# Two interleaved chains of a sequence model: three more handover points, one lead, and issue-order edges for the last causal convolution

## The chip, the core and the metric

The program runs on one core of a Trainium2 chip. The metric is device time in microseconds (us) from start to end of one execution. All data are 32-bit floats. The engines are named as in the profile: PE is TensorE (matrix products), DVE is VectorE, ACT is ScalarE, POOL is GpSimd, SP is SyncE, which here only issues transfers (DMA).

## The reference

The input x has 4 sequences of 512 steps, each step a vector of D = 128 x 64 = 8192. Two layers follow each other. Cut to what matters, with the layer norm written as `ln` and the learned scales left out:

```python
# layer 0, for each sequence
xn = ln(x);  k, v, r = xn @ Wk, xn @ Wv, sigmoid(xn @ Wr)     # 8192 -> 64
s[t] = decay * s[t-1] + k[t] * v[t]                           # scan over time
x = x + (r * s) @ Wo                                          # 64 -> 8192
x = x + gelu(conv3_over_128(ln(x)) + freq_b)                  # 'SAME'
x = x + ln(causal_depthwise_conv3_over_time(ln(x)) + time_b)  # three taps
x = x + gelu(x @ W1 + b1) @ W2 + b2                           # 64 -> 256 -> 64
# layer 1
trend = moving_average(x, 25);  X = rfft(x - trend)[:128]     # over time
y = trend + irfft(einsum(X, complex W per channel))
```

Every `ln` is over all 8192 values of a time step, so its mean and variance are known only when the last channel has been seen.

## The kernel before, in words

Layer 0 holds channels on partitions and the 512 steps in the free dimension. The 8192 channels make 64 tiles of 128, handled in 32 *pairs* (`NPR = 32`), so a tile named `x1`, `z`, `kd` and so on is 128 x 2 x 512. Per sequence `b` there are these stages, each a Python generator that emits instructions and yields a weight:

- **J** `project` (L325): k, v, r and the first statistics, two yields a pair. For b > 1 the weights of two pairs come in one transfer (L351) into a buffer `wx`, of which there are two. `scale_weights` (L355) multiplies them by the norm's scale on DVE (L358). For pair 0 this is free for the planner to place; for later pairs it is tied by `keep_in_program_order`.
- **Z** `scan` (L420): first the statistics of the step (L428 to L433, the last of them on POOL, L234), then `rows` (L281), which spreads a column of 512 values over all partitions by four matmuls (L242) and copies it out on ACT (L286), once for `rs` and once for the mean. Then two products `pk` (L470), one product `pr` (L478), the sigmoid (ACT, L485), the scan (DVE, L489), `rst` (DVE, L491), the product `pq` with `rst` (L496), and a last group `pe` (L504, L505) with the statistics after it. A `yield CHAIN` stands between these groups.
- **A** `attend_and_convolve` (L515): for each pair `attend` (L529 to L535), `convolve` (L550 to L570) and two pairs later `add_up` (L252), the sums for the next statistics. At the end `finish` (L257: the sums copied to s_sb on ACT, `yield CHAIN`, eight small matmuls L264) and `moments` (L272, with POOL's L233 and L234).
- **C** `convolve_time` (L646): `rows`, then for each pair `normed` (two DVE operations, L613 and L616), `tapped` (two ACT L621, four DVE L625, one POOL L631, a store) and its square; PE only has `add_up`, two steps later. Then `finish` and `moments` again. For b = 1 and 2 the first 14 pairs (`AHEAD`) were already made by `convolve_ahead` (L634), inside F of the sequence before.
- **O** `open_feed` (L706): `rows` and the first two residual pairs.
- **F** `feed_forward` (L714): for each pair four quarters `q`, each with one `widen` (L732, gelu on ACT L737) and one `narrow` (L745), then DVE's L758, which empties the two accumulators `p` and `pb` (one bank each, so the next pair's `narrow` waits for it), and a pair or two later `store` (L764, copies L772 and L777). DVE also makes `residual` (L691, L692) and `add_residual` (L703) of the pair two ahead.

**Who sets the order.** PE runs in the order in which the generators emit. `in_turn` (L823) runs two chains, k = 0 and k = 1, side by side through eight pairs of stages (L867 to L874). Each chain has a place `at[k]`: n for the pair of stages, plus a fraction that grows with each yield by weight x share / `whole[stage]`. Chain 1 moves when `at[1] < at[0] + lead`, otherwise chain 0; `lead` runs linearly from `leads[n]` to `leads[n + 1]`. When a stage ends within an entry such as `(C, 0.95), (O, 0.05)`, the generator `run` goes straight on into the next stage; a handover happens only at a yield. `feed_forward` yields after each quarter while the other chain is in a step it called narrow (`CHAIN`), otherwise after each pair.

The queues of DVE, ACT, POOL and SP are ordered by a planner when the program is built: in a simulated run it gives each engine, of what is ready, the instruction that was emitted first. `tc.keep_in_program_order(i)` (in L344, L360, L615, L629, L700) adds one edge: `i` is issued after the instruction emitted just before it on the same engine.[...]

**Layer 1** (L879) starts when layer 0 has ended: transforms, mixing, inverse transforms. The change does not touch it.

Of the kernel before, what the change touches and what calls it, by code (L numbers as in the profile page):

```python
# [24 lines left out]
NPR = NCH // 2  # L25
# [21 lines left out]
def conv_seq_kernel(  # L47
# [26 lines left out]
    x4 = [dram.tile([T, D], F32, tag=f"x4_{b}", name=f"x4_{b}") for b in range(B)]  # L74

    layer0(tc, dram, x, xt, vecs, wkvr, wo, wdec, wconv, fbias, w1, fb1, w2, fb2, x4)
    layer1(tc, x4, wri, dftv, dftd, dfte, idfte, idfto, avg, avgh, out)


@with_exitstack  # L80
def layer0(ctx, tc, dram, x, xt, vecs, wkvr, wo, wdec, wconv, fbias, w1, fb1, w2, fb2, x4):
# [5 lines left out]
    B = x.shape[0]  # L87
# [17 lines left out]
    def two(pool, tag):  # L105
        return pool.tile([P, 2, SL], F32, tag=tag, name=tag)
# [125 lines left out]
    def rsqrt(rs, var):  # L232
        nc.gpsimd.tensor_scalar(rs, var, EPS, None, ALU.add)  # L233
        nc.gpsimd.tensor_tensor(rs, rs, mhalf, ALU.pow)  # L234

    def cols(name):
        return tiny.tile([P, NT], F32, tag=name, name=name)

    def spread(ps, col):

        for t in range(NT):
            nc.tensor.matmul(  # L242
                ps[:, t * P : (t + 1) * P], lhsT=col[:, t : t + 1].to_broadcast([P, P]), rhs=ident,
                start=True, stop=True,
            )

    def add_up(st, i, pair, squares, first, last):

        for j in range(2):
            for k, src in ((0, pair), (1, squares)):  # L250
                q = 2 * j + k
                nc.tensor.matmul(  # L252
                    st[32 * q : 32 * q + 32, :], lhsT=ones, rhs=src[:, j, :],
                    start=first, stop=last,
                )

    def finish(st, bank, tag):  # L257

        s_sb = rowp.tile([P, SL], F32, tag="s", name="s_sb")
        nc.scalar.copy(s_sb, st)  # L260
        yield CHAIN
        pm = bank()
        for t in range(NT):
            nc.tensor.matmul(  # L264
                pm[:, 2 * t : 2 * t + 2], lhsT=s_sb[:, t * P : (t + 1) * P], rhs=pick,
                start=True, stop=True,
            )
        me = tiny.tile([P, NT, 2], F32, tag=f"me{tag}", name="me")
        nc.vector.tensor_copy(me.rearrange("p t k -> p (t k)"), pm[:, 0 : 2 * NT])
        return me[:, :, 0], me[:, :, 1]  # L270

    def moments(mean, square, tag):  # L272

        var, rs, mrs = cols(f"var{tag}"), cols(f"rs{tag}"), cols(f"mrs{tag}")
        nc.vector.tensor_tensor(var, mean, mean, ALU.mult)
        nc.vector.tensor_tensor(var, square, var, ALU.subtract)
        rsqrt(rs, var)
        nc.vector.tensor_tensor(mrs, mean, rs, ALU.mult)
        return rs, mrs

    def rows(bank, a, b, names):  # L281
        both = rowp.tile([P, 2, SL], F32, tag=names, name=names)
        for k, col in enumerate((a, b)):
            pb = bank()
            spread(pb, col)
            nc.scalar.copy(both[:, k, :], pb)  # L286
            yield CHAIN
        return both[:, 0, :], both[:, 1, :]

    def pair_of(row):  # L290
        return row.unsqueeze(1).to_broadcast([P, 2, SL])
# [6 lines left out]
    def spare(tag, n):  # L298
        return fr.tile([P, 2, n], F32, tag=tag, name=tag, bufs={"z": 4, "wx": 2}.get(tag, 3))
# [120 lines left out]
    def scan(b):  # L420
# [13 lines left out]
        if b == 0:  # L434
# [25 lines left out]
            nc.vector.tensor_copy(qo[S:P, 0:S], pq[S:P, 0:S])  # L460
            nc.vector.tensor_scalar_mul(qo[S:P, S:], pq[S:P, S + 2 :], 1.0 / D)
        gw, bw, qo = sums["gw"], sums["bw"], sums["qo"]
        rb, mb = yield from rows(bank, rs, mean, "rm" if b > 1 else "rm3")
        if b == 0:
            kv = two(fr, "x1")
# [138 lines left out]
    def fetch(tag, src, b, i):  # L604
        t = bk.tile([P, 2, SL], F32, tag=tag, name=tag, bufs=3 if tag == "kx" else 2)
        nc.sync.dma_start(t, src[b][2 * i : 2 * i + 2].rearrange("c p t -> p c t"))
        return t


    def normed(b, i, x2, xr, rb, mb, pinned=False):  # L610

        nc.sync.dma_start(x2, x2d[b][2 * i : 2 * i + 2].rearrange("c p t -> p c t"))
        first = nc.vector.tensor_tensor(xr, x2, pair_of(rb), ALU.mult)  # L613
        if pinned:
            tc.keep_in_program_order(first)  # L615
        nc.vector.tensor_tensor(xr, xr, pair_of(mb), ALU.subtract)  # L616

    def tapped(b, i, xr, to, pinned=False):
        for j in range(2):
            c = slice(2 * i + j, 2 * i + j + 1)  # L620
            nc.scalar.activation(  # L621
                to[:, j, :], xr[:, j, :], AF.Identity, bias=tb_all[:, c], scale=vec[:, W2, c]
            )
            for k, w in ((1, W1), (2, W0)):
                tap = nc.vector.scalar_tensor_tensor(  # L625
                    to[:, j, k:], xr[:, j, : SL - k], vec[:, w, c], to[:, j, k:], ALU.mult, ALU.add
                )
                if pinned and j == 0 and k == 1:
                    tc.keep_in_program_order(tap)  # L629
        cc = slice(2 * i, 2 * i + 2)  # L630
        nc.gpsimd.tensor_tensor(to[:, :, 0:2], to[:, :, 0:2], fix[:, cc, :], ALU.add)  # L631
        nc.gpsimd.dma_start(tod[b][cc].rearrange("c p t -> p c t"), to)
# [13 lines left out]
    def convolve_time(b):  # L646
        bank = of_a if b == B - 1 else of_p
        made = AHEAD if b in ahead else 0
        moment = carried.pop(b)
        if made:  # L650
            rb, mb = ahead.pop(b)
        else:
            rb, mb = yield from rows(bank, *moment, "rm" if b == B - 1 else "rm3")
        st = bank()
        waiting, added = [], 0
        n = NPR - made
        for k in range(n + 2):
            while waiting and waiting[0][0] == k - 2:
                add_up(st, 0, *waiting.pop(0)[1:], added == 0, added == NPR - 1)
                added += 1  # L660
            if k < n:
                if b == B - 1:

                    x2, xr, to, sq = spare("xp", SL), spare("x1", SL), spare("z", SL), two(bk, "sq")
                else:
                    x2 = bk.tile([P, 2, SL], F32, tag="kx", name="x2", bufs=3)
                    xr, to = two(bk, "kd"), bk.tile([P, 2, SL], F32, tag="k3", name="to", bufs=3)
                    sq = bk.tile([P, 2, SL], F32, tag="sq4", name="sq4", bufs=2)

                normed(b, made + k, x2, xr, rb, mb, made > 0 and k < 4)  # L670
                tapped(b, made + k, xr, to)
                nc.scalar.activation(sq, to, AF.Square)
                waiting.append((k, to, sq))
                i = k * made // n
                if i != (k + 1) * made // n:

                    to = fetch("kh", tod, b, i)
                    sq = bk.tile([P, 2, SL], F32, tag="mid", name="sq5", bufs=4)
                    nc.scalar.activation(sq, to, AF.Square)
                    waiting.append((k, to, sq))  # L680
            yield 7.0 * (NPR + 2) / (n + 2)
        mean, sq = yield from finish(st, bank, 4)
        causal[b] = moments(mean, sq, 4)


    def residual(b, i):
# [123 lines left out]
    CHAIN = 6.0  # L810
# [40 lines left out]
    def nothing(b):  # L851
        yield 1.0

    J, Z, A, C, O, F = project, scan, attend_and_convolve, convolve_time, open_feed, feed_forward
    begin[A] = 0
    needed = {A: scanned, C: carried, O: causal, F: opened}
    whole = {
        J: 2.0 * NPR, Z: 7 * CHAIN, A: 7.0 * NPR + 3 * CHAIN, C: 7.0 * (NPR + 2) + 3 * CHAIN, O: 4 * CHAIN,
        F: 9.0 * (NPR + 1), nothing: 1.0,
    }  # L860
    with tc.manual_schedule(engines={nc.tensor.engine}):
        for _ in project(0):
            pass
        prepare()
        in_turn(
            (0.12, 0.12, 0.08, 0.1, 0.08, 0.1, -0.05, 0.08, 0.0),
            ((0, (Z, 0.12), (A, 0.88)), (1, (J, 0.88), (Z, 0.12))),  # L867
            ((0, (C, 1.0)), (1, (A, 1.0))),
            ((0, (O, 0.05), (F, 0.95)), (2, (J, 0.88), (Z, 0.12))),
            ((1, (C, 1.0)), (2, (A, 1.0))),  # L870
            ((1, (O, 0.05), (F, 0.95)), (3, (J, 0.88), (Z, 0.12))),
            ((2, (C, 1.0)), (3, (A, 1.0))),
            ((2, (O, 0.05), (F, 0.95)), (3, (C, 0.95), (O, 0.05))),
            ((3, (F, 1.0)), (3, (nothing, 1.0))),  # L874
        )
# [321 lines left out]
```

## Time and profile before

| | |
|---|---|
| three runs | 3748.67, 3748.59, 3736.15 us; median 3748.59 |
| the profiled execution | 3734.79 us, its span from first to last instruction 3733.0 us |
| mean granted PE clock | 0.981 |
| layer 0 ends (last `store`) | about 2752 us |

The stretches of layer 0, from the windows of the profile, with the stages that run side by side (n is the pair of stages):

| n | stretch, us | stages | PE busy, us | DVE busy, us |
|---|---|---|---|---|
| 0 | 210 to 520 | A0 with J1, Z1 | 298.35 | 173.47 |
| 1 | 520 to 795 | C0 with A1 | 251.14 | 262.29 |
| 2 | 795 to 1225 | O0, F0 with J2, Z2 | 404.51 | 293.35 |
| 3 | 1225 to 1450 | C1 with A2 | 215.80 | 200.93 |
| 4 | 1450 to 1890 | O1, F1 with J3, Z3 | 418.24 | 300.22 |
| 5 | 1890 to 2122 | C2 with A3 | 223.87 | 200.43 |
| 6 | 2122 to 2487 | F2 with C3, O3 | 323.70 | 326.00 |
| 7 | 2487 to 2752 | F3 | 262.22 | 150.49 |

A line of the timeline gives the start, the time from start to end, the engine, the line of the kernel, the operation, output<-inputs, their shapes and how many instructions are merged; in brackets stands how long the engine had been idle before it and what ended that. A 32-bit matmul of the program shows as two PE instructions.

### The profile page before, as it was taken

What the parts mean: (1) busy time and instruction counts of PE and PEld (TensorE: products, weight loads), DVE (VectorE), ACT (ScalarE), POOL (GpSimd) and SP (SyncE); (2) the same over time, 40 slices, a digit from 0 to 9 for tenths busy, and PEclk for the clock granted to TensorE, in tenths of its full rate; (3) what the DMA queues carried; (4) which work ended last, traced back from release to release, by engine and by line L of the source; (5) the groups of instructions that cost most, each with busy time, mean ns of one, the idle gap of its engine ahead of it and who ended that gap; (6) DMA issues with size and microseconds to landing.
All of it is one profiled execution on the core that took longest, in us unless ns stands there. A gap on an engine that the chain in (4) does not pass through costs nothing. (4 is left out here: it accounts for less than half of the span.)

```text
span 3733.0 us, 53000 instructions
## 1 busy us (share of the span) xinstructions
PE 3521.2 (94%) x20041; PEld 1360.6 (36%) x20041; DVE 2671.9 (72%) x3498; ACT 1778.0 (48%) x2331; POOL 447.3 (12%) x654
## 2 busy tenths in 40 slices
PE   9999999999998999999989989999989999989998
PEld 4433322234333223433322233333323843328533
DVE  4455569976776896676789699946658277792677
ACT  0012346655656565565656578868854200152100
POOL 0000012210101221001122122100000000001000
PEclk9999999999999999999999999999999999999999
DMA  9867657787874687788578677645569478894687
GB/s 314 279 211 242 227 177 262 260 276 265 290 262 168 235 280 271 266 292 278 182 238 286 213 247 267 234 149 196 198 203 287 150 240 290 290 297 164 213 294 260
DMA packets 427223, 910.29 MB, mean 244 GB/s; under 512 B 32728, under 2 KB 83160, under 8 KB 422872
## 3 DMA queue, kind: packets, MB, share of 16 engines
q1 hardware_dynamic: 353136, 636.92, 52.5%
q0 software_dynamic: 71680, 268.46, 19.7%
q8 instruction: 160, 2.62, 0.3%
q10 hardware_dynamic: 2152, 1.51, 0.1%
q14 instruction: 95, 0.78, 0.1%
HBM read 638.26 MB, written 268.50 MB: 243 GB/s over the span
## 5 line engine op out<-in xcount | busy, mean ns | idle before, releaser
L745 PE MATMUL p<-mid,w_sb 64*64 64x512 f32 x2048 | 554.5, 599 | 20.3 <-DVE wx L758 20.3
L745 PE MATMUL pb<-mid,w_sb 64*64 64x512 f32 x2048 | 536.2, 598 | 0.0
L737 ACT ACTIVATE mid<-c,fb_sb 128x1024 f32<-128x1024 f32 x256 | 284.3, 1111 | 97.2 <-PE c L732 94.8
L737 ACT ACTIVATE mid<-m,fb_sb 128x1024 f32<-128x1024 f32 x256 | 284.6, 1112 | 93.5 <-PE m L732 92.1
L732 PE MATMUL c<-x,w_sb 64*64 64x512 f32 x2016 | 281.2, 611 | 13.2 <-ACT mid L737 6.9
L732 PE MATMUL m<-x,w_sb 64*64 64x512 f32 x2016 | 283.0, 612 | 6.7 <-ACT ob L777 4.9
L745 PEld LDWEIGHTS p<-mid,w_sb 64*64 64x64 f32 x2048 | 155.5, 135 | 294.9 <-issue 262.0
L409 PE MATMUL a<-xp,wx 128*128 128x512 f32 x512 | 242.6, 617 | 9.1 <-DVE wx L358 8.6
L1043 ACT COPY two<-a 128x512 f32<-128x512 f32 x64 | 37.5, 585 | 428.9 <-PE a L1038 428.9
L1066 PE MATMUL b<-xin,avg_sb 128*128 128x512 f32 x512 | 230.8, 593 | 3.3 <-DVE xin L1072 3.3
L1072 DVE TENSOR_TENSOR xin<-b,pm 128x512 f32<-128x512 f32 x256 | 159.1, 683 | 100.2 <-PE b L1069 85.3
L570 ACT ACTIVATE sq<-x 128x1024 f32<-128x1024 f32 x128 | 135.1, 1055 | 181.4 <-DVE x L567 181.3
L625 DVE SCALAR_TENSOR_TENSOR to<-kd,vec,to 128x510 f32<-128x510 f32 (+1 forms) x272 | 197.1, 744 | 9.8 <-ACT to L621 8.7
L700 ACT ACTIVATE kd<-kd,vec 128x512 f32<-128x512 f32 x256 | 192.8, 803 | 3.1 <-DVE kd L692 3.1
L252 PE MATMUL st<-x,ones 128*32 128x512 f32 x512 | 176.8, 603 | 13.1 <-DVE x L567 13.1
L925 DVE COPY xf<-b 128x256 f32<-128x256 f32 x128 | 54.4, 425 | 178.3 <-PE b L1012 169.4
L625 DVE SCALAR_TENSOR_TENSOR z<-x,vec,z 128x511 f32<-128x511 f32 x240 | 175.9, 745 | 5.3 <-ACT z L621 3.0
L531 DVE TENSOR_TENSOR x<-a,xp 128x1024 f32<-128x1024 f32 x128 | 156.1, 1220 | 30.6 <-PE a L529 28.4
L703 DVE TENSOR_TENSOR x<-kd,kx 128x1024 f32<-128x1024 f32 x126 | 154.1, 1223 | 32.8 <-ACT kd L700 32.7
L529 PE MATMUL a<-rst,wo_sb 64*128 64x512 f32 x512 | 147.0, 648 | 27.1 <-DVE x L531 25.1
L758 DVE SCALAR_TENSOR_TENSOR x4t<-p,fb_sb,x 128x512 f32<-128x512 f32 x64 | 47.9, 748 | 172.0 <-PE pb L745 169.6
L692 DVE TENSOR_TENSOR kd<-kd,rm 128x1024 f32<-128x1024 f32 x128 | 155.7, 1220 | 7.8 <-ACT rm L286 6.3
(269 smaller groups left out, 6755.1 us busy)
## 6 DMA issues: line engine op xcount, KB each, us to landing
xp<-in_xt SPq DMA_DIRECT2D x256, 512.0 KB
kh<-to SPq DMA_DIRECT2D x156, 512.0 KB
x<-x POOLq DMA_DIRECT2D x128, 512.0 KB, 4.6
kx<-x SPq DMA_DIRECT2D x128, 512.0 KB
x<-ob POOLq DMA_DIRECT2D x64, 1024.0 KB, 8.0
xin<-x SPq DMA_DIRECT2D x64, 1024.0 KB
out<-xin POOLq DMA_DIRECT2D x64, 1024.0 KB, 6.6
x<-x SPq DMA_DIRECT2D x96, 512.0 KB
```

The lines of the kernel that those rows point to most:

```text
L252: nc.tensor.matmul(st[32 * q : 32 * q + 32, :], lhsT=ones, rhs=src[:, j, :], start=first, stop=last,)
L409: nc.tensor.matmul(pa[:, k, :], lhsT=wq[:, j, k * P : (k + 1) * P], rhs=xp[:, j, :], start=first and j == 0, stop=last and j == 1,)
L531: nc.vector.tensor_tensor(x1, at, xp, ALU.add)
L625: tap = nc.vector.scalar_tensor_tensor(to[:, j, k:], xr[:, j, : SL - k], vec[:, w, c], to[:, j, k:], ALU.mult, ALU.add)
L692: nc.vector.tensor_tensor(d, d, pair_of(mb), ALU.subtract)
L700: tc.keep_in_program_order(nc.scalar.activation(d[:, j, :], d[:, j, :], AF.Identity, bias=vec[:, B4, c], scale=vec[:, G4, c]))
L703: nc.vector.tensor_tensor(x3, d, x2, ALU.add)
L732: nc.tensor.matmul(pm[halves[j], h, :], lhsT=w1_sb[halves[h], q * H : (q + 1) * H], rhs=x3[halves[h], j, :], start=True, stop=True,)
L737: nc.scalar.activation(mid, pm, AF.Gelu_apprx_tanh, bias=fb1_sb[:, q : q + 1])
L745: nc.tensor.matmul(sums2[i][j][halves[h], :], lhsT=w2_sb[halves[j], q, :], rhs=mid[halves[j], h, :], start=q == 0, stop=q == 3,)
L1066: nc.tensor.matmul(po[j], lhsT=avg_sb[:, j, :], rhs=xin[:, j, :], start=True, stop=False)
L1072: nc.vector.tensor_tensor(by_n(xin[:, j, :]), by_n(po[j]), by_c(pm[j % 2][:, j // 2, :]), ALU.add)
```

## The change

Four edits:

1. In `convolve_time`, `normed` and `tapped` of the last sequence (b = 3) get `keep_in_program_order` on their first DVE instruction (the first of the taps in `tapped`); in `normed` the condition `made > 0` stays in front.
2. In `scan`, a `yield CHAIN` between the statistics and `rows`; in `convolve_time`, a `yield CHAIN` after the last `moments`.
3. `whole` counts the new yields: Z has 8 instead of 7, C has 4 instead of 3.
4. The lead at the border from pair 5 to pair 6 goes from -0.05 to -0.1.

```diff
         gw, bw, qo = sums["gw"], sums["bw"], sums["qo"]
+        yield CHAIN
         rb, mb = yield from rows(bank, rs, mean, "rm" if b > 1 else "rm3")
...
-                normed(b, made + k, x2, xr, rb, mb, made > 0 and k < 4)
-                tapped(b, made + k, xr, to)
+                normed(b, made + k, x2, xr, rb, mb, made > 0 and (k < 4 or b == B - 1))
+                tapped(b, made + k, xr, to, b == B - 1)
...
         causal[b] = moments(mean, sq, 4)
+        yield CHAIN
...
-        J: 2.0 * NPR, Z: 7 * CHAIN, A: 7.0 * NPR + 3 * CHAIN, C: 7.0 * (NPR + 2) + 3 * CHAIN, O: 4 * CHAIN,
+        J: 2.0 * NPR, Z: 8 * CHAIN, A: 7.0 * NPR + 3 * CHAIN, C: 7.0 * (NPR + 2) + 4 * CHAIN, O: 4 * CHAIN,
...
-            (0.12, 0.12, 0.08, 0.1, 0.08, 0.1, -0.05, 0.08, 0.0),
+            (0.12, 0.12, 0.08, 0.1, 0.08, 0.1, -0.1, 0.08, 0.0),
```

## The prediction

> **What bounds the kernel now.** I read the page's busy times first, then PE's waits, the windows, and PE's and DVE's timelines where the waits lie.
>
> ```profile
> PE 3521.2 (94%) x20041; PEld 1360.6 (36%) x20041; DVE 2671.9 (72%) x3498; ACT 1778.0 (48%) x2331; POOL 447.3 (12%) x654
> PE p L745 <- DVE wx L758: 20.3, 7, 5.8
> PE a L242 <- POOL rs L234: 12.3, 6, 4.0
> PE p L242 <- POOL rs L234: 4.2, 2, 2.1
> ```
>
> PE is busy 94%: a step that is reordered pays only by idle time of PE. The waits (total, times, longest) say what the handovers can reach: the spreads of `rows` wait for POOL's L234 16.5 us in all, in eight places. Where they are, in PE's timeline:
>
> ```profile
> 810.57 1.85 PE L242 MATMUL p<-ident,rs 128*128 128x128 f32 x8 [2.08 <-POOL rs L234]
> 1141.94 1.16 PE L242 MATMUL a<-ident,rs 128*128 128x128 f32 x8 [1.91 <-POOL rs L234]
> 1807.68 1.16 PE L242 MATMUL a<-ident,rs 128*128 128x128 f32 x8 [1.63 <-POOL rs L234]
> 2127.19 2.07 PE L242 MATMUL a<-ident,rs 128*128 128x128 f32 x8 [3.41 <-POOL rs L234]
> 2460.93 2.08 PE L242 MATMUL a<-ident,rs 128*128 128x128 f32 x8 [4.03 <-POOL rs L234]
> 2462.80 1.92 PE L764 MATMUL m<-ident,wx 128*128 128x128 f32 x8
> ```
>
> These are O0, Z2, Z3, C3 and O3; the other three, at C0, A1 and A0, follow `moments` of A or the end of Z, where nothing is added. After the longest waits PE runs at half speed: the spread takes 2.08 us instead of 1.16, the transposes 1.92 instead of 1.09.
>
> Pair 6 is different, as the windows show (length, then PE, PEld, DVE, ACT, POOL busy, the granted PE clock, the DMA share, GB/s):
>
> ```profile
> 2300.00:2350.00 50.00, 45.17 (x372) 17.25 (x368) 49.69 (x58) 43.23 (x54) 9.68 (x13) 0.97 0.80 257
> 2600.00:2650.00 50.00, 50.00 (x448) 19.51 (x444) 30.51 (x30) 41.20 (x46) 2.27 (x3) 1.00 0.59 198
> ```
>
> While C3 runs beside F2, DVE is full (49.69 of 50) and PE waits for it now and then; when F runs alone PE is full. Removing a wait of PE in the first kind of window gains nothing by itself.
>
> [...] The trace agrees on the half (above), and shows it after 2.31 us of idleness too (1833.62: the next L732 group takes 1.97 us, not 1.04). [...] at 1174.15 below, ready DVE work stands behind one that waits. [...] the trace has 1.28 before the sigmoid L485.
>
> **The change, part by part.** I worked `in_turn` through with both sets of fractions to see which emission moves.
>
> *The edges: nothing.* `made` is 14 only for b = 1 and 2, so for b = 3 `made > 0` is false and `normed` is not tied. In `tapped` the instruction emitted just before the first tap is L616 of the same pair, whose output the tap reads. The edge is there already. 0 us; no reason for a gain or loss.
>
> *Z0.* One half-step of J1 goes between statistics and spread. The idle time there is 0.73 us (180.88, waiting for DVE L461), but J1 waits 3.65 us for its weights at 192.56, which may eat it: -0.4, from -0.7 to 0.
>
> *Z1.* No idle time at its spread now: no gain. But its later steps move. Z's steps were 0.12/7 = 0.0171, and are 0.015. Chain 1 starts at 0.88, so `pr` is emitted at 0.955 and `pq` at 0.97; with lead 0.12 they need at[0] > 0.835 and > 0.85. A's steps (0.88/242 a unit weight) take at[0] from 0.833 to 0.851 in one `convolve`: both conditions come true at once, and `pr` and `pq` stand next to each other. Before, an `attend` and a `convolve` (some 5 us) lay between, and still:
>
> ```profile
> 467.47 0.74 DVE L483 SCALAR_TENSOR_TENSOR rg<-rm,gw,p 128x512 f32<-128x512 f32 x1
> 470.92 1.22 DVE L489 TENSOR_TENSOR_SCAN state<-decb,wx 128x512 f32<-128x512 f32 x1
> 473.17 0.69 DVE L491 TENSOR_TENSOR rst<-rg,state 128x512 f32<-128x512 f32 x1
> 473.91 1.07 PE L496 MATMUL p<-rst,qo 64*64 64x512 f32 x2 [2.02 <-DVE rst L491]
> ```
>
> `pr` ended at 467.1, `rst` at 473.86: 6.8 us with L531 and L535 between. DVE's own operations are 0.74 + 0.69 + 0.48 + 0.74 + 1.22 + 0.69 = 4.6; with one foreign one (1.1) 5.7 us of idle PE, and some 2.2 us from the half clock (after 4.03 at 2460.93 three groups took 5.9 us instead of 3.3, 2.6 more). 7.9 - 2.0 = +5.9, from 0 to +9. Everything of A0 and A1 is queued behind `pq` on PE.
>
> *C0 to O0.* A half-step of J2 (four products of the program, about 2 us) comes between `moments` and the spread: -2.0 of 2.08, from -2.1 to 0. For C1 to O1 there was no wait. A step of C shrinks from 7/256 to 7/262 of the stage, so C runs slightly further ahead of A in pairs 1, 3, 5; DVE does the same work, 0.
>
> *Z2.* A `store` and a quarter of F0 (over 3 us) cover its spread: -1.9. There is a second effect, in DVE's queue:
>
> ```profile
> 1169.50 1.22 DVE L489 TENSOR_TENSOR_SCAN state<-decb,wx 128x512 f32<-128x512 f32 x1
> 1174.15 0.55 DVE L358 TENSOR_SCALAR wx<-wx,vec 128x192 f32<-128x192 f32 x2 [3.42 <-DMA wx<-in_wkvr]
> 1174.61 0.74 DVE L758 SCALAR_TENSOR_TENSOR x4t<-p,fb_sb,x 128x512 f32<-128x512 f32 x1
> 1175.50 1.09 PE L764 MATMUL c<-ident,x4t 128*128 128x128 f32 x4 [4.71 <-DVE x4t L758]
> ```
>
> L358 here scales the weights of J3's pair 2, nearly 300 us before J3: it is tied to that of pair 1, which is tied to that of pair 0, which is free, so all three float up. It waits for a transfer into the `wx` buffer that the scan held till L489, and PE waits behind L758. With the new fractions the `moments` of C1 (DVE's L278) are emitted just before pair 2's scaling; the tie then holds it to its place. L758 would start near 1170.8 and leave about 0.95 us of PE idleness, as at the later stores (1201.55). Gain 4.71 - 0.95, the second wait of 0.61, and about 1.9 of half clock: -6.3. The transfer itself is still issued and may hold SP's queue. Against it, `pr` to `pq` have only two quarters (4.3 us) between them instead of a `store` and two: `rst` needs 0.7 + 0.7 on DVE, a table load 1.28 and the sigmoid 0.72 on ACT, 0.7 on DVE, waits and one or two foreign operations: 6.5 us, so +2.2. Sum -6.0, from -8.2 to 0.
>
> *Z3.* -1.6 at the spread, and +1.4 at `pq` (2.2 where 0.77 is now): -0.2, from -3 to +4.
>
> *The border and pair 6.* With the lead at -0.1, O2's `rows` and the first pair and a quarter of F2 come before A3's last `moments`. What PE now idles for A3's statistics at 2122.73 (0.71) goes. But `moments` of A3 and the spread of C3 stay adjacent (A ends without a yield), so the 3.41 stays, later: F2 starts at 2122 instead of 2129, C3's DVE work not at 2130.7 but after two `widen`, 1.5 us for the gelu, five quarters of 2.15, L264, the 3.41 and the spread: near 2142.5. From there I count DVE: successive starts in the timeline are 1.13 us for a 1024-wide operation (three L616 from 2137.82 take 3.50 us together) and 0.66 for a tap, so a C3 pair is 2 x 1.13 + 4 x 0.67 = 4.94, a pair of F2 3 x 1.13 + 2 x 0.66 = 4.73. An F2 pair outside the overlap costs PE's 8.93 us (80 instructions a pair at 448 in 50 us). Before: 24 pairs of F2 have their L758 by 2399, so 2130.7 + 32 x 4.94 + 24 x 4.73 + 8 x 8.93 = 2473.7. After: C3's steps run at 1.33 a pair instead of 1.2 and end one pair of F2 earlier, so 21.7 pairs overlap, 1.25 lie ahead: 2142.5 + 158.1 + 102.6 + 80.8 = 2484.0. +10.3. The waits at L745 in this stage (20.3 us) are DVE being full, and I count no gain there. Fewer `add_up` stand in F2's tail (its pairs take 9.5 there, now 8.93): -1.2. And O3: two quarters, a `store` and another quarter cover its statistics: -4.0 and -2.6 of half clock. Sum +2.5, from -8 to +10.
>
> **Sum:** -0.4 + 5.9 - 2.0 - 6.0 - 0.2 + 2.5 = -0.2 us. On the profiled execution, 3734.8 us (span 3733.0 and 1.8 around it), that is 3734.6. The three runs lie at 3748.6 twice and 3736.2; their mean is 3744.5, the median 4 us higher. I predict 3744. The bounds of the terms add to -22 and +23: 3722 to 3767.
>
> **Rivals.** *A, most of the idleness goes.* If the planner reorders DVE in pair 6 so that L758 never waits, all that the handovers and the lead can touch is gone: 2.1 + 1.9 + 1.6 + 0.7 + 3.4 + 4.0, 6.3 at Z2, L745's waits at the border 3.72 + 5.83, and some 8 of half clock: -37.5, and Z1 doesn't grow: 3707. For it: those waits are long. Against: DVE at 49.69 of 50.
> *B, C3 comes late (slower).* DVE is the bound of pair 6, and each F2 pair pushed out of the overlap costs 8.93 - 4.73 = 4.2 us. My +10.3 counts 2.3 such. Five more are +21 and the sum +20.8: 3765. It decides (over 0.5%) from 18.9 / 4.2 = 4.5 pairs beyond mine, that is with C3's first L613 past 2142.5 + 4.5 x 8.93 = 2183; with Z1 at its upper bound from 3.8. For it: the last `moments` of A3 need three small DVE slots among F2's work. Against: they are emitted early and so come first. C3's loads (L612 on SP) also stand behind those of three more F2 residuals (L606), and its stores (L632 on POOL) come later; I count 0 for both, as loads run pairs ahead and the transfer share is 0.80 there; if that cover fails, L613 waits for its load and this rival has its cause.
> *C, all is hidden anyway:* the moved waits reappear at the next wait (J's weights, `p`'s bank), and Z1's five microseconds are taken from A0's own waits: 3745.
>
> Chances: forecast 0.57, A 0.2, B 0.11, C 0.12. Since 0.5% (18.7 us) is about what a measurement of this kernel can tell from no change, forecast and C count as the same: 0.69; faster 0.2, slower 0.11. The range takes the bounds, a little of A: 3720 to 3765.
>
> **What would show it.** `pq` of Z1 with 5 to 6 us of idleness; no L358 waiting near 1174; no wait at the spreads of Z2, Z3, O0, O3; one of about 3.4 us at C3, after a pair of F2; C3's L613 near 2142; DVE's order within a C3 pair unchanged. The prediction is wrong if `pr` and `pq` are apart in PE's order, if L758 in pair 6 stops waiting, or if F2's end moves by more than 10 us.

## The result, and the profile after

The changed kernel takes 3754.9 us (median of 9 runs, 3749.6 to 3758.6), the kernel before 3737.2 beside it (9 runs, 3726.4 to 3748.7). The ratio is 1.0035, with a 95% interval of 1.0022 to 1.0048: 13.1 us slower, 8.2 to 17.9. (The medians alone lie 17.7 us apart; the text uses the ratio on record.) The profiled execution took 3749.6 (span 3747.8), 14.8 more than that of before. The handovers are two new yields, although the title counts three.

The busy times of the page and the waits of PE (total, times, longest) after the change:

```profile
PE 3530.2 (94%) x20041; PEld 1358.5 (36%) x20041; DVE 2670.0 (71%) x3498; ACT 1781.6 (48%) x2331; POOL 447.1 (12%) x654
PE st L252 <- DVE x L568: 19.6, 21, 3.7
PE p L747 <- DVE wx L760: 18.3, 7, 4.3
PE m L734 <- ACT mid L739: 10.8, 8, 6.4
PE p L497 <- DVE rst L492: 6.9, 1, 6.9
PE a L242 <- POOL rs L234: 5.0, 3, 3.8
PE p L242 <- POOL rs L234: 2.4, 2, 2.1
```

The code lines have moved by one from the scan on and by two after the convolution (L745 is L747 now, L758 is L760). The spreads of `rows` wait 7.4 us instead of 16.5: the handovers did what they say. But new rows stand beside them: `pq` of Z1 waits 6.9 us, the column sums `st` of A 6.5 us more than before (13.1), and `widen` waits 10.8 us for ACT at its bank `m`, where it was 1.6, most of it in F2. L747's wait for DVE (L760) has hardly changed. PE's timeline at the places that the prediction showed, in order Z1, Z2, Z3, A3's end, C3's spread, F2:

```profile
478.15 1.96 PE L497 MATMUL p<-rst,qo 64*64 64x512 f32 x2 [6.88 <-DVE rst L492]
1145.25 1.00 PE L766 MATMUL c<-ident,x4t 128*128 128x128 f32 x6 [1.53 <-DVE x4t L760]
1173.57 0.66 PE L766 MATMUL c<-ident,x4t 128*128 128x128 f32 x2 [5.93 <-DVE x4t L760]
1807.06 1.11 PE L766 MATMUL c<-ident,x4t 128*128 128x128 f32 x7 [1.53 <-DVE x4t L760]
1832.73 1.23 PE L766 MATMUL c<-ident,x4t 128*128 128x128 f32 x8 [3.29 <-DVE x4t L760]
2132.05 1.91 PE L252 MATMUL st<-x,ones 128*32 128x512 f32 x2 [3.71 <-DVE x L568]
2152.66 2.07 PE L242 MATMUL a<-ident,rs 128*128 128x128 f32 x8 [3.76 <-POOL rs L234]
2180.69 1.13 PE L734 MATMUL m<-x,w_sb 64*64 64x512 f32 x4 [6.37 <-ACT mid L739]
```

No spread of O0, Z2, Z3 or O3 waits any more; at Z2 and Z3 a wait of 1.53 us at the next `store` stands in its place. C3's spread waits about as long as before (3.76 us for 3.41), 25 us later. In the windows of pair 6 nothing is new, DVE is full while C3 runs (49.69 of 50) and PE when it has ended:

```profile
2300.00:2350.00 50.00, 44.20 (x356) 18.07 (x360) 49.69 (x57) 41.47 (x51) 9.70 (x13) 0.97 0.78 257
2600.00:2650.00 50.00, 49.82 (x444) 19.36 (x440) 31.27 (x32) 40.72 (x47) 2.36 (x4) 1.00 0.56 191
```

To see where the time went I took, in both traces, the time from the start of an instruction of PE to that of a later one (the k-th of its kind), how much of it PE idled, and how much the halved clock took (half of the stretches in it with a granted clock of 0.5). The table gives the differences to the kernel before, and already those of the three single parts from the experiments below: total (idle, clock).

| stretch | after | scan alone | convolution alone | lead alone |
|---|---|---|---|---|
| A0's attend 24 to A1's attend 8 (with Z1) | +10.6 (+4.9, +6.8) | +7.5 (+4.9, +5.1) | +12.8 (0, +15.4) | 0 (0, 0) |
| J2's start to F0's first narrow (O0) | -4.6 (-1.8, -1.7) | -1.7 (0, -1.7) | -4.6 (-1.8, -1.7) | 0 |
| F0's pair 24 to J3's start (Z2, pair 3) | -3.5 (-1.9, -6.8) | -4.3 (-2.7, -5.1) | -3.6 (-2.5, -6.8) | -3.8 (-0.2, -5.1) |
| F1's pair 24 to A3's attend 0 (Z3) | +0.7 (+0.5, 0) | +0.7 (+0.4, 0) | +0.4 (+0.5, 0) | 0 |
| A3's attend 0 to its last convolve (pair 5) | +9.4 (-0.8, +5.1) | +1.5 (-0.9, +5.1) | +7.0 (-1.2, +12.0) | +10.5 (+2.7, +5.1) |
| from there to F2's first narrow | -4.1 (-1.1, 0) | 0 | -0.2 (+0.4, -1.7) | -5.1 (-0.7, -1.7) |
| F2's pairs 0 to 15 | +18.9 (+10.7, +5.1) | +0.1 | +3.3 (+1.9, 0) | +15.9 (+8.1, +6.8) |
| F2's pairs 16 to 31 (with O3) | -6.4 (-4.1, -3.4) | -1.6 (-0.1, -1.7) | -10.8 (-6.7, -3.4) | -3.8 (-3.1, -1.7) |

Rows five and six belong together: after the change, and with the lead alone, O2's rows are emitted ahead of A3's last convolve and so count in row five. The clock column has to be read with care: the convolution alone loses 15.4 us at Z1, where its instructions are those of the kernel before, and the lead alone has -3.8 in row three, where it changes nothing. What that is comes first among the experiments.

### The profile page after: what moved, and what is told of

It is laid out like the page before. It is cut to its first block, busy times and chain, and to the rows that moved or that the text cites. A ratio compares the mean times of both kernels' runs of the same rounds, so it can differ in the third digit from the quotient of the medians.

```text
span 3747.8 us, 52999 instructions
## 1 busy us (share of the span) xinstructions
PE 3530.2 (94%) x20041; PEld 1358.5 (36%) x20041; DVE 2670.0 (71%) x3498; ACT 1781.6 (48%) x2331; POOL 447.1 (12%) x654
## 5 line engine op out<-in xcount | busy, mean ns | idle before, releaser
L747 PE MATMUL p<-mid,w_sb 64*64 64x512 f32 x2048 | 558.7, 600 | 19.1 <-DVE wx L760 18.3
L747 PE MATMUL pb<-mid,w_sb 64*64 64x512 f32 x2048 | 534.6, 599 | 0.0
L734 PE MATMUL m<-x,w_sb 64*64 64x512 f32 x2016 | 280.3, 610 | 15.5 <-ACT mid L739 10.8
L734 PE MATMUL c<-x,w_sb 64*64 64x512 f32 x2016 | 280.9, 611 | 10.8 <-ACT mid L739 7.3
L747 PEld LDWEIGHTS p<-mid,w_sb 64*64 64x64 f32 x2048 | 156.8, 135 | 292.7 <-issue 257.8
L626 DVE SCALAR_TENSOR_TENSOR to<-kd,vec,to 128x511 f32<-128x511 f32 (+1 forms) x272 | 195.9, 749 | 9.4 <-ACT to L622 8.4
L760 DVE SCALAR_TENSOR_TENSOR x4t<-p,fb_sb,x 128x512 f32<-128x512 f32 x64 | 47.9, 748 | 182.7 <-PE pb L747 182.7
L569 POOL DMA_DIRECT2D x<-x x128 | 93.6, 731 | 568.9 <-DVE x L568 558.9
```

The lines of the kernel that those rows point to most:

```text
L626: tap = nc.vector.scalar_tensor_tensor(to[:, j, k:], xr[:, j, : SL - k], vec[:, w, c], to[:, j, k:], ALU.mult, ALU.add)
L734: nc.tensor.matmul(pm[halves[j], h, :], lhsT=w1_sb[halves[h], q * H : (q + 1) * H], rhs=x3[halves[h], j, :], start=True, stop=True,)
L747: nc.tensor.matmul(sums2[i][j][halves[h], :], lhsT=w2_sb[halves[j], q, :], rhs=mid[halves[j], h, :], start=q == 0, stop=q == 3,)
```

## The experiments

Ratios are to the kernel before, run beside each; in us they are multiplied by 3739. My theory before the experiments: the loss sits in two places, at Z1 (the scan's handover) and at the border of pairs 5 and 6 (the lead). The rival: it is all in pair 6, where DVE is full.

**The edges alone.**

```diff
-normed(b, made + k, x2, xr, rb, mb, made > 0 and k < 4)
-tapped(b, made + k, xr, to)
+normed(b, made + k, x2, xr, rb, mb, made > 0 and (k < 4 or b == B - 1))
+tapped(b, made + k, xr, to, b == B - 1)
```

> The two edges alone. Both theories: the instruction order of every engine is that of the kernel before, so the ratio is 1.000; what it differs by, and where the two traces part by chance of the granted clock, is what a difference of a few us means in this study (expected: within 0.1%, 4 us, and single profiles apart by up to 7 us).

Measured 0.9998 (0.9986 to 1.0009). The instructions of all five engines are the same and in the same order, so this is a second profile of the kernel before. Yet in pair 5 it is 3.7 us longer, with 5.1 us more lost to the clock and 0.6 us less idle. That is the size of chance in one profile and one stretch. In pair 5 it is one-sided: the traces of seven kernels in which DVE has the same order there as before (the edges, the scan, its two halves, and below C3's handover, that without C2, and C3's spread covered) are all 1.5 to 4.9 us longer from A3's attend 0 to its last convolve. The profile of the kernel before is a fast one there, and some 3 us of each figure for pair 5 belong to that. Chance can be larger. Windows of the kernel before, and then of the convolution alone, at the end of Z1 (length, PE, PEld, DVE, ACT, POOL, granted clock, DMA share, GB/s):

```profile
474.00:504.00 30.00, 27.55 (x157) 9.78 (x158) 15.24 (x20) 11.20 (x17) 4.34 (x6) 1.00 0.40 134
```

```profile
474.00:504.00 30.00, 28.06 (x100) 9.23 (x101) 10.08 (x17) 6.21 (x9) 2.78 (x4) 0.60 0.28 92
```

The pause before both is the same, 2.02 us at `pq` (473.91 and 474.16), in the same order of work. In one execution the clock stays whole, in the other it is halved for 13.65 us and soon again for 10.24, and the 30 us hold 100 matmuls instead of 157. So single profiles serve here for idle time and its place, and the runs for sums.

**The three parts, each alone.**

```diff
+        yield CHAIN                    # scan, ahead of rows
-Z: 7 * CHAIN
+Z: 8 * CHAIN
```

> The handover in scan alone (Z counted as 8 steps). Theory 1 (the loss sits at Z1 and at the border of pairs 5 and 6): +9.5 us stand by the end of chain Z1, nothing at O0 and O3, the spreads of Z2 and Z3 give back 1 to 2 us each, the long wait at the identity copies of x4t in Z2 for the third weight pair stays; sum +6 to +9, ratio 1.0016 to 1.0024. Theory 2 (the loss is all in pair 6, where DVE is full; what stands at Z1 is eaten later): -2 to +2 us at the end.

```diff
+        yield CHAIN                    # convolve_time, after moments
-C: 7.0 * (NPR + 2) + 3 * CHAIN
+C: 7.0 * (NPR + 2) + 4 * CHAIN
```

> The handover after a convolution's moments alone (C counted with 4 chain steps). Theory 1: -4 us at O0, -5 at Z2 (the third pair's scaling no longer waits on DVE ahead of the store's), -6 to -8 at O3, pair 6 otherwise as before; sum -12 to -18, ratio 0.9952 to 0.9968. Theory 2: C's smaller steps put more of C's DVE work beside F2 late, PE's waits at the narrow products grow by 10 us or more in pair 6; sum 0 to +5.

```diff
-(0.12, 0.12, 0.08, 0.1, 0.08, 0.1, -0.05, 0.08, 0.0)
+(0.12, 0.12, 0.08, 0.1, 0.08, 0.1, -0.1, 0.08, 0.0)
```

> The lead of -0.1 at the border of pairs 5 and 6 alone. Theory 1: A3's end shows an idle PE of 3 to 4 us at the column sums of its last pair (no spread of O2 left to cover it), the 3.4 us wait at C3's spread stays, and F2's tail ends later; +6 to +12 us, ratio 1.0016 to 1.0032, all of it after 2100 us. Theory 2: +12 to +18 us, most of it in waits of PE for ACT or DVE within F2's first five pairs.

| part | ratio (95%) | us | my prediction's terms |
|---|---|---|---|
| scan | 1.0015 (1.0005 to 1.0025) | +5.6 | -0.4 + 5.9 - 1.9 + 2.2 - 0.2 = +5.6 |
| convolution | 0.9977 (0.9966 to 0.9989) | -8.6 | -2.0 - 6.3 - 6.6 = -14.9 |
| lead | 1.0044 (1.0031 to 1.0057) | +16.5 | +10.3 - 1.2 = +9.1 |

Edges and parts together are +12.8, the change +13.1: on the whole they add up. The scan's term held as a sum (that it fits to the tenth is luck, the interval is 1.9 to 9.3, and of its parts Z2 went another way, below), the lead costs nearly twice what I had, and the convolution gives 6 us less. Of the expectations, the scan came just under theory 1's range; the convolution fell between the two, and theory 2's growing waits are not there; the lead's 16.5 lies in theory 2's range, not in mine, although theory 1's idle PE at A3's sums is in its trace (3.71 us).

**Scan's two halves.** The handover for b < 2 only, with eight steps for these two chains, and for b > 1 only, with seven as before:

```diff
+        if b < 2:                      # the other kernel: if b > 1
+            yield CHAIN
-weight * share / whole[stage]
+weight * share / (8 * CHAIN if stage is scan and b < 2 else whole[stage])    # b < 2 only
```

> The handover in scan for b < 2 only, with eight steps for these two chains and seven for Z2 and Z3 as before. Theory 1: Z1's pq shows 6 to 7 us of idle PE and half clock after it; +5 to +9 us, ratio 1.0013 to 1.0024. Theory 2: -1 to +2 us, ratio 0.9997 to 1.0005.

Measured 1.0022 (1.0009 to 1.0036), +8.2 us: theory 1. `pq` of Z1 in its timeline, and then what DVE did in the changed kernel between `pr`'s end (471.25) and `rst`:

```profile
480.97 1.96 PE L498 MATMUL p<-rst,qo 64*64 64x512 f32 x2 [7.17 <-DVE rst L493]
```

```profile
471.25 1.21 DVE L490 TENSOR_TENSOR_SCAN state<-decb,wx 128x512 f32<-128x512 f32 x1
472.39 0.72 DVE L484 SCALAR_TENSOR_TENSOR rg<-rm,gw,p 128x512 f32<-128x512 f32 x1
473.03 1.21 DVE L568 TENSOR_TENSOR x<-m,x 128x1024 f32<-128x1024 f32 x1
474.16 0.68 DVE L485 TENSOR_TENSOR rg<-rg,rm 128x512 f32<-128x512 f32 x1
475.83 0.55 DVE L358 TENSOR_SCALAR wx<-wx,vec 128x192 f32<-128x192 f32 x2 [0.99 <-DMA wx<-in_wkvr]
477.40 0.69 DVE L492 TENSOR_TENSOR rst<-rg,state 128x512 f32<-128x512 f32 x1 [1.02 <-ACT rg L486]
```

One foreign operation (L568), as I had counted, and the sigmoid's way over ACT, which I had not put into Z1's sum: L358 with its 0.99 us of waiting fits into that. PE idles 6.88 us instead of the 5.7 forecast.

> The handover in scan for b > 1 only, Z's steps as before, nothing else. Theory 1 (scan's loss is Z1, where pr and pq become neighbours): -1 to -4 us, ratio 0.9989 to 0.9997. Theory 2 (in Z2 and Z3 the wait at the spread comes back at the identity copies of x4t and at ACT's mid, with more behind it): +3 to +8 us, ratio 1.0008 to 1.0021.

Measured 1.0035 (1.0018 to 1.0052), +13.1 us, above both theories. This kernel is not what the change does to Z2 and Z3: with eight steps of a seventh each the chain ends later, and A's spread comes right behind it. Its timeline at Z3:

```profile
1840.77 1.97 PE L766 MATMUL m<-ident,x4t 128*128 128x128 f32 x8 [4.40 <-ACT mid L739]
1854.27 2.08 PE L242 MATMUL a<-ident,rs 128*128 128x128 f32 x8 [2.09 <-POOL rs L234]
```

The trace has +5.6 us at Z3 (idle +2.8, clock +5.1); its runs have the lowest mean clock of all (0.976, before 0.980). So the share per step matters too, not the handover alone. The same edit on top of the convolution's:

> The handover after a convolution's moments, and that in scan for b > 1 only, with Z's steps as before: Z0 and Z1 are emitted as in the kernel before, the lead is -0.05, no edges. Theory 1: the convolution's -8.6 and 1 to 4 us at Z2 and Z3: -9 to -13 us, ratio 0.9965 to 0.9976. Theory 2 (Z2 and Z3 have nothing to give once the convolution hands over): -8.6 us, ratio 0.9977.

1.0002 (0.9990 to 1.0014): both theories missed, the handover at this share takes back what the convolution's gave.

**The change without the lead.**

```diff
-(0.12, 0.12, 0.08, 0.1, 0.08, 0.1, -0.1, 0.08, 0.0)
+(0.12, 0.12, 0.08, 0.1, 0.08, 0.1, -0.05, 0.08, 0.0)     # rest as changed
```

> The whole change except the lead, which stays at -0.05. Theory 1 (the parts add up; the lead is the loss): +5.6 for scan and -8.6 for the convolution, together -3 us, ratio 0.9987 to 0.9997. Theory 2 (the two handovers give back part of each other's gain in pair 6): +3 to +8 us, ratio 1.0008 to 1.0021.

Measured 1.0010 (0.9995 to 1.0024), +3.7 us: at the low end of theory 2's range; the interval (-1.9 to +9.0) just reaches theory 1's. Theory 2's reason is not in the trace: from A3's last convolve to F3 it has -9.2 us, the whole gain. Against the change's 1.0035 that leaves 9 us, give or take 7, for the lead in the company of the rest.

**The lead's two halves.** `in_turn` interpolates: `lead = leads[n] + (leads[n + 1] - leads[n]) * (at[0] - n)`. The entry for the border is also the end of pair 5's slope, so C2's pairs are emitted up to two of A3's `convolve` earlier. My prediction had looked at the border only.

```diff
+            if n == 5:
+                lead -= 0.05 * (at[0] - 5)       # pair 5 only
```

> The lead is interpolated over pair 5 towards its value at the border, so -0.1 also shifts C2 against A3 all through pair 5. Here only that part: the lead goes to -0.1 over pair 5, and pair 6 has its old leads. Theory 1 (half of the lead's cost lies in pair 5, where DVE's order changes from A3's attend 8 on): +5 to +9 us, ratio 1.0013 to 1.0024. Theory 2 (all of it lies at the border and in pair 6): -1 to +3 us, ratio 0.9997 to 1.0008.

```diff
+            if n == 6:
+                lead -= 0.05 * (7 - at[0])       # pair 6 only
```

> The other part: pair 5 has its old lead up to -0.05, and pair 6 starts at -0.1. Emission at the border and in pair 6 as with the whole lead. Theory 1: +5 to +10 us, ratio 1.0013 to 1.0027 (C3 starts some 16 us late against A3's end, and pair 6 ends 7 to 9 later). Theory 2: +14 to +18 us, ratio 1.0037 to 1.0048.

Pair 5 alone: 1.0019 (1.0010 to 1.0029), +7.1 us, theory 1. Its trace has +8.0 from A3's attend 0 to its last convolve (idle +2.0, clock +3.4), some 3 of it chance as above, and nothing at the border. DVE takes C2's work in another order, and one `attend` of A3 waits longer for L531, 3.14 us instead of 2.09:

```profile
1949.85 1.13 PE L529 MATMUL a<-rst,wo_sb 64*128 64x512 f32 x4 [3.14 <-DVE x L531]
```

That is not the loss, though: all waits of `attend` for L531 in this stretch take 7.2 us here and 7.4 before, and in the changed kernel PE idles 0.8 us less in pair 5 than before. So the 7.1 us are shown by the runs; in which wait they lie is not shown.

Pair 6 alone: 1.0036 (1.0022 to 1.0050), +13.5 us, just under theory 2's range. Its trace has +7.2 from A3's last convolve to F3, and +6.7 before it, where O2's rows now stand right behind C2's `moments`, with a halved clock after the pause (the second spread takes 2.08 us, the first 1.16; some 3 us are the chance in pair 5, and the next stretch, which has lost O2's rows, is 4.9 shorter):

```profile
2111.38 1.16 PE L242 MATMUL p<-ident,rs 128*128 128x128 f32 x8 [2.10 <-POOL rs L234]
2113.21 2.08 PE L242 MATMUL p<-ident,mrs 128*128 128x128 f32 x8 [0.68 <-ACT rm L286]
```

The 2.10 us are this kernel's own: with the whole lead, alone or in the change, C2 ends earlier and O2's first spread doesn't wait (its second waits 0.71 us, as before). The two halves, 7.1 and 13.5, therefore need not add to the lead's 16.5; what is left of it beside pair 5 is 9.4.

**What a late C3 costs.** Three more kernels move the border. In the first, O2's rows wait under the full lead until A3's last convolve is emitted; in the second the lead is 0; in the third (with the convolution's handover for C3 alone, below) C3 yields once before its rows, so that a whole pair of F2 covers its spread.

```diff
+        while b == B - 2 and not summed[0]:      # open_feed; summed is set after A3's last convolve
+            yield BLOCKED
```

> The lead of -0.1 alone, but O2's rows are held back until A3's last convolve is emitted, so that its spreads and residuals cover A3's last column sums again, as before the change. Theory 1 (C3 starts late and its work on DVE ends late, and that is the price): at most the 3.7 us of idle PE and some 2 us of half clock go, +10 to +14 us remain, ratio 1.0027 to 1.0037. Theory 2 (A3's uncovered sums and the clock after them are the price): +2 to +6 us, ratio 1.0005 to 1.0016.

```diff
-(0.12, 0.12, 0.08, 0.1, 0.08, 0.1, -0.05, 0.08, 0.0)
+(0.12, 0.12, 0.08, 0.1, 0.08, 0.1, 0.0, 0.08, 0.0)
```

> The kernel before with a lead of 0 at the border instead of -0.05: A3's end and C3's rows come ahead of O2's residuals and of F2. Theory 1 (every us by which C3 starts later costs about one): C3 starts 5 to 8 us earlier against A3's end, -3 to -7 us, ratio 0.9981 to 0.9992. Theory 2 (the order at the border itself decides, and -0.05 is where O2 covers A3's sums): A3's sums and both spreads stand bare, +3 to +8 us, ratio 1.0008 to 1.0021.

```diff
+            if b == B - 1:                       # convolve_time, ahead of rows
+                yield BLOCKED
```

> The handover for C3 alone, and C3 yields once before its rows, so that a whole pair of F2 stands on PE between A3's last statistics and C3's spread; C3's first pair keeps its place in PE's order, the lead is -0.05. Theory 1 (the bare spread is worth its 3.4 us and some 2 us of half clock, and C3's later first pair costs at most one pair of F2 outside the overlap, 4.2 us): -9 to -13 us against the kernel before, ratio 0.9965 to 0.9976. Theory 2 (every us by which C3 starts later is lost again in pair 6): -3 to -7 us, ratio 0.9981 to 0.9992.

Holding O2 back: 1.0049 (1.0030 to 1.0069), +18.3, theory 1 or worse. A lead of 0: 1.0034 (1.0019 to 1.0049), +12.7, on theory 2's side and above its range. C3's spread covered: 1.0001 (0.9989 to 1.0012), +0.4, worse than both theories and 8 us behind the same kernel without that yield. From the traces, us after the start of the last bias product of A3's last convolve:

| kernel | C3's first `normed` on DVE | F2's first narrow | F3's first narrow |
|---|---|---|---|
| before | 16.8 | 19.4 | 376.8 |
| C3's handover | 16.8 | 19.4 | 367.5 |
| the same, C3's spread covered | 26.9 | 17.3 | 376.8 |
| lead, pair 6 only | 30.7 | 14.5 | 383.9 |
| lead alone | 30.6 | 14.3 | 383.7 |
| lead, O2 held back | 33.4 | 17.2 | 386.5 |
| lead of 0 | 21.0 | 29.1 | 383.5 |
| changed kernel | 31.6 | 15.3 | 385.2 |

Rows two and three differ in C3's rows alone: C3 10.1 us later, the end 9.3 us later, although the spread doesn't wait any more:

```profile
2141.48 1.16 PE L242 MATMUL a<-ident,rs 128*128 128x128 f32 x8
2161.18 1.99 PE L736 MATMUL c<-x,w_sb 64*64 64x512 f32 x8 [6.09 <-ACT mid L741]
```

So an early C3 was worth more than the 3.4 us of idle PE at its spread, and of the two theories the second has the right sign. DVE shows why. From that bias product to C3's last tap it is idle for 8.8 us with C3's handover and for 15.3 with the spread covered, and C3 ends 6.5 us later. In the kernel before it is idle for 12.5, with the lead alone for 28.2, and C3 ends 11.0 us later. A us of delay isn't worth the same everywhere: here 10.1 cost 9.3 at F3, with the lead alone 13.8 cost 7.0. Nor was the cover free of new waits: 2.20 us at F2's first `widen`, for O2's residual, and one at C3's second spread:

```profile
2143.87 1.16 PE L242 MATMUL a<-ident,mrs 128*128 128x128 f32 x8 [1.23 <-ACT rm L286]
```

Holding O2 back was to show what A3's 3.71 us cost, and doesn't: O2's spreads do cover A3's sums there, but F2's first `widen` then waits for O2's residual instead, so the idle time has only moved:

```profile
2129.95 1.99 PE L736 MATMUL m<-x,w_sb 64*64 64x512 f32 x8 [3.96 <-DVE x L705]
```

With the lead of 0 theory 1's premise fails: C3 starts 4 us later there, as O2's spreads are emitted between A3's end and C3's, and F2 starts 10 us late as well.

**Where 6 us of the convolution's gain went.**

```diff
+        if b == 3:                     # the others: b == 2; b != 2
+            yield CHAIN
-weight * share / whole[stage]
+weight * share / (whole[stage] + CHAIN * (stage is convolve_time and b == 3))
```

> The convolution's handover for C3 alone (only C3 has four chain steps). Theory 1 (the gain at O3 is whole, and something in pair 5 takes part of the convolution's gain): pair 6 gives -7 to -9 us, ratio 0.9976 to 0.9981. Theory 2 (the gains themselves were over-sized): -2 to -5 us, ratio 0.9987 to 0.9995.

> The convolution's handover for C2 alone. Nothing waits at O2, so there is nothing to gain; C2's smaller steps bring it forward against A3, by half as much as the lead's slope over pair 5 does. Theory 1 (that costs, as the slope did): +3 to +7 us, ratio 1.0008 to 1.0019. Theory 2 (pair 5 cost nothing here, its clock loss was chance): -2 to +2 us, ratio 0.9995 to 1.0005.

> The convolution's handover for C0, C1 and C3, not C2. Theory 1: -4.6 at O0, -3.6 at Z2 and -7.7 in pair 6, without pair 5's loss: -12 to -16 us, ratio 0.9957 to 0.9968. Theory 2: -7 to -10 us, ratio 0.9973 to 0.9981, as the handover for all four.

C3 alone: 0.9979 (0.9970 to 0.9988), -7.9 us, theory 1: O3's term (-6.6) is real. Its trace has no wait at O3, and -9.2 us from F2's first narrow to F3's:

```profile
2463.39 1.16 PE L242 MATMUL a<-ident,rs 128*128 128x128 f32 x8
```

C2 alone: 1.0007 (0.9997 to 1.0018), +2.6 us, which tells nothing from no change. C0, C1 and C3: 0.9979 (0.9968 to 0.9989), theory 2: no more than C3 alone. Its trace shows -4.6 at O0 and -3.8 at Z2, but the lead alone and C2 alone, which change nothing at Z2, show -3.8 and -3.5 there too; PE idles 1.8 us less at O0 and 0.9 less at Z2. So what O0 and Z2 save isn't found in the runs, though the two intervals leave room for some 5 us. C2's steps don't explain it, nor does the clock: its mean over the runs is 0.981 with these three handovers, 0.980 with C3's alone and 0.979 before. Whether another wait takes it back stays open. The handover for C3 alone is faster than both kernels.

## Why the prediction was wrong

No change was forecast (-0.2 us), and the change costs 13.1. Two steps failed. What the lead does over pair 5 was put at nothing, and alone it measured +7.1; what is left of the lead's 16.5, 9.4, is close to the 9.1 that I had for the border. And the -8.3 forecast for the convolution's handover at O0 and in DVE's queue at Z2 is not found: the handover for all four convolutions gives -8.6, for C3 alone -7.9. That 3754.9 lies inside the stated range is no merit; the range was 45 us wide.

*Edges: right.* Same order, 0.9998.

*Z0 and Z1, +5.5: right in kind and nearly in size.* The two chains alone cost +8.2 (3.4 to 13.5), with the pause at `pq` that was forecast (5.7, measured 6.88).

*C0 to O0, -2.0:* the wait is gone in every trace with this handover. What it brings in the runs isn't shown (above).

*Z2, -6.0: the way wrong, the sum not found in the runs.* The spread no longer waits, and from F0's pair 24 to Z2's end the trace has -5.0 (-3.5 up to J3's start); by chance alone the edges' trace has +1.5 there. But "leaves about 0.95 us of PE idleness" failed: 5.93 us stand at 1173.57. L358 still floats up and waits 1.65 us for its transfer, the chain's operations follow it, and only then L760. `pq` needed no wait (+2.2 forecast). With the convolution's handover alone the pause is 1.36 us, as I had argued.

*Z3, -0.2: right* (+0.7; 3.29 us at 1832.73 instead of 2.31, the spread free).

*Pair 5, 0: this step failed.* I had written that C runs slightly further ahead of A in pairs 1, 3 and 5 and that DVE does the same work, with C's smaller steps in mind; C2's steps alone, +2.6 (-1.1 to 6.7), can't be told from that 0. But the lead's slope brings C2 forward too, and I had not counted it as part of the lead at all. The lead's half in pair 5 alone costs +7.1 (3.7 to 10.8). DVE does the same work in another order; which wait makes that dear stays open, and in the company of the other edits pair 5 was not run apart.

*Border and pair 6, +2.5: the late C3 was sized well, two other steps were wrong.* Forecast was C3 11.8 us later against A3's end and +10.3; measured 13.8 to 14.8 later and +7.0 in the lead's trace, or, with nothing else moved, 10.1 later and +9.3. But "what PE now idles for A3's statistics goes" turned into 3.71 us: O2's spreads had covered A3's last sums before. What that costs isn't shown, as the kernel that covers them again waits elsewhere. And O3's -6.6 was added as if it didn't depend on the late C3. From A3's last convolve to F3 the changed kernel's trace stands at +8.4, the lead alone at +7.0, the convolution alone at -7.7, so in the traces that gain is gone; the runs, in which the parts add up, don't confirm it. This stays open; with the lead alone O3 waits only 2.10 us. F2's end, which was to move by no more than 10 us, moved by 18.4 (F3's first narrow from 2490.65 to 2509.02).
C3's first `normed`, forecast near 2142, came at 2155.39, with A3's end itself 9.9 us later than before:

```profile
2155.39 1.23 DVE L614 TENSOR_TENSOR x<-xp,rm 128x1024 f32<-128x1024 f32 x1 [2.59 <-ACT rm L286]
```

*The rivals.* A fell: L760 waits as before (18.3 us for 20.3). B, the late C3, had the right mechanism, but its deciding point (2183) wasn't reached; the loss is that mechanism at its small size plus pair 5. C fell as a whole with the runs of the parts; at O0 and Z2 it may hold. I had held 18.7 us to be what a measurement can tell from no change; these nine runs tell 5. The sum of -0.2 missed +13.1 by a gain 6 us too large (the convolution) and a cost 7 us too small (the lead).

## What to carry to other kernels

A number in a schedule that is interpolated acts over the whole stage before its place: work an edit of it through on every engine's order from the last fixed value on, not only where it stands. Where a full engine sets the end of a stage, as DVE did here (49.69 us of 50), an early start of its work is worth more than a covered wait: 10 us of delay cost 9 in one pair of kernels here and 14 cost 7 in another, more than the 3.4 us of visible idleness at stake. Where one pause of 2.02 us is followed by a halved clock and another isn't, as at Z1 here, compare idle times between single traces, and take sums from many runs. And see whether an experiment that removes a wait has only moved it.

## What the runs showed of the hardware

In the traces of the kernel before and of the changed one TensorE's clock is either whole or halved (granted 1.0 or 0.5). The halved stretches, but for the last, which each trace's end cuts short, take 3.41, 6.83, 10.24, 13.65 or 17.07 us, multiples of 3.41. In either trace all changes of the clock lie on one grid of 3.413 us (51 and 55 changes, none more than 0.001 off), whose first point is 1.89 us after the start of the span in the one and 1.26 in the other. From 150 to 3700 us of both traces, 35 steps of the grid at whole clock had 2.0 us or more of idle PE in them, and all 35 were followed by a halved one; with 1.8 to 2.0 us it was 8 of 12, with less than 0.6 us 2 of 1799. The two profiles at Z1 agree with this: the pause of 2.02 us at `pq` lies in one step with the convolution alone (clock halved from its end on), and in the kernel before it is cut by the grid into 1.04 and 0.98 us (clock whole). Two more pauses of the kernel before part in the same way: the one of 2.08 us that ends at 810.57 lies in one step, and the clock is halved from 810.85 on; the one of 2.10 us that ends at 535.46 is cut into 1.01 and 1.09, and the clock stays whole. So for these four pauses near 2 us it was their place on the grid that went with the clock after them, not their length. Why the halved stretch at Z1 lasted 13.65 us with the convolution alone isn't shown.

The kernel before lies between 3725 and 3756 us in 69 runs, at mean clocks of 0.984 to 0.973; over these runs 0.001 of mean clock goes with 2.2 us.
